# A graph network on one core: edge places computed in two pieces, and another division of labour for the masks of the second attention

## The chip, the cores and the metric

The kernel runs on one core of one Trainium2 chip. A core has a matrix engine (TensorE, PE in the profile; its weight loads are PEld), a vector engine (VectorE, DVE), a scalar engine (ScalarE, ACT), a general engine (GpSimd, POOL), a queue processor for transfers (SyncE, SP) and 16 DMA engines. The metric is the time of one execution on the device in microseconds.

## The reference, cut to what matters

There are 3125 nodes with 128 features, and 100,000 edges (`src`, `dst`, a weight, a type), sorted by `dst`. Four graph layers follow one another, each with a norm before it and a residual. The change touches what prepares the edges for all of them, and layer 0, two graph attentions:

```python
def gat_layer(x, W, a_s, a_d, b, src, dst):          # H = 4 heads of C = 32
    h = (x @ W).reshape(-1, H, C)
    al_src = jnp.einsum('nhc,hc->nh', h, a_s)
    al_dst = jnp.einsum('nhc,hc->nh', h, a_d)
    e = jax.nn.leaky_relu(al_src[src] + al_dst[dst], 0.2)
    m = jax.ops.segment_max(e, dst, num_segments=N)
    ...
    w = jnp.exp(e - m[dst])
    denom = jax.ops.segment_sum(w, dst, num_segments=N)
    alpha = w / jnp.maximum(denom[dst], 1e-16)
    out = jax.ops.segment_sum(h[src] * alpha[:, :, None], dst, num_segments=N)
    return out.reshape(-1, H * C) + b
x = jax.nn.relu(gat_layer(x, W1, a_src1, a_dst1, b1, src, dst))
x = jax.nn.relu(gat_layer(x, W2, a_src2, a_dst2, b2, src, dst))
```

## The kernel before, in words

**Blocks.** Nodes are cut into 25 blocks of 128 (`NB`). The edges become a dense matrix of edge counts, `counts` (source in the partition, target in the column, fp8), which stays in SBUF, and one of weights in DRAM. Gathers and segment sums are then matrix products.

**Placing the edges** (`place_edges`, L924 on). The edges are laid out as 112 partitions of 896 edges (`EC`; seven pieces of 128, `EK`). VectorE works out for each edge a row of a table in DRAM, so that the edges between one source block and one target block stand together: it compares the edge's block numbers, and a loop over 13 pairs of source blocks (L1019 to L1025: make a mask, scan along the row with a carry from the partition above, copy where the mask is set) gives the edge's rank among its like. Integer steps (L1027 to L1041) make the place `lane` out of it, with `cap` and `base`, two functions of the target block (L998 to L1011). L1043 to L1048 replace the places by plain numbers if the input is not as assumed; the test is a matrix product with ones into `ps_small`. Transposes (L1050 to L1056) make `idx` of it, the edge records are transposed into `rec` (L1058 to L1075), and GpSimd then issues 782 indirect transfers (L1081; the page's `table<-rec,idx`) of 128 edges each, one for each chunk `c` in the order `ORDER`, which begins with the chunks of target block 5. VectorE goes on with sums per target block (L1091), and `src` and `dst` are written out in another layout (L1113 to L1115).

**Building the graph and the first attention.** `graph_and_layer0` (L1376) interleaves, for the groups of blocks in `GROUPS` (blocks 5 to 24 in fours, then 0 to 2, then 3 and 4), `build_block` for each block with `attend(1, ...)` for the group. `build_block` loads the block's part of the table as soon as the scatters that can hold its edges are done, makes one-hot matrices on VectorE (L1174, L1176) and multiplies them (L1188, L1191).

**Attention on a group** (`attend`, L1318). The softmax's exponentials are products of a factor of the source and one of the target, with one pair of factors where the sum of the two scores is above zero and another where it is below. So for each head, source block `sb` and group, a mask `over` is made, the counts where `row > minus[sb]` and zero elsewhere: `row` is the targets' score, laid along the free axis in PSUM by TensorE transposes (`row_of`, tile `ps_row`), and `minus` holds the source's negated score, one per partition. TensorE multiplies each mask with the source's `parts` (L1349) into `ps_acc` over all 25 source blocks. Afterwards VectorE sums the three bf16 parts (L1354: the head's final sums), and a chain of VectorE operations (L1360 to L1373) at the end of the group makes the output. The same sum without a mask, `u`, comes from L1331 and L1333.

The second attention runs `attend(2, ...)` over five groups of five blocks (masks of 128x640), the first over the seven groups of `GROUPS` (128x512 at most). In the second, 6 of the 25 masks (`sb % 4 == 2`) are made by GpSimd in two operations, compare (L1341, `above`) and multiply (L1343); since GpSimd does not read PSUM here, `row_of` has ScalarE copy the row into SBUF (L1449). All other masks are one VectorE operation (L1346), which reads `ps_row` itself.

Each engine works in the order in which the kernel was written down, by the tile framework's semaphores: instructions on different engines that touch the same tile wait for one another, two readers of one PSUM tile included.

Of the kernel before, what the change touches and what calls it, by code (L numbers as in the profile page):

```python
# [7 lines left out]
F32 = mybir.dt.float32  # L8
# [51 lines left out]
FIRST = 5  # L60
ORDER = list(range(LOW[FIRST], ROWS)) + list(range(LOW[FIRST]))
GROUPS = [(q, q + 4) for q in range(FIRST, NB, 4)] + [(0, 3), (3, 5)]
# [836 lines left out]
class FastGnn(Gnn):  # L899
# [24 lines left out]
    def place_edges(self, placed):  # L924
# [9 lines left out]
        with ExitStack() as s:  # L934
# [63 lines left out]
            nc.scalar.copy(sb, sb_i)  # L998
            cap, base, step = tile("cap"), tile("base"), tile("step")
            V.tensor_scalar(cap, db, 24.0, 8.0, op0=OP.is_gt, op1=OP.mult)  # L1000
            V.tensor_scalar(cap, cap, 1.0, None, op0=OP.add)
            V.tensor_scalar(base, db, float(N_SLOTS[-1]), None, op0=OP.mult)
            for d in range(NB - 1):
                for _ in range(CAP[d] - CAP[d + 1]):
                    V.scalar_tensor_tensor(cap, db, d + 0.5, cap, op0=OP.is_lt, op1=OP.add)
                more = N_SLOTS[d] - N_SLOTS[d + 1]
                if more:
                    V.tensor_scalar(step, db, d + 1.0, float(more), op0=OP.min, op1=OP.mult)
                    V.tensor_add(base, base, step)
            V.tensor_tensor(step, sb, cap, op=OP.mult)  # L1010
            V.tensor_add(base, base, step)  # L1011

            left, wrong = tile("left"), work.tile([A, 2], F32, name="wrong")
            d0, d1 = tile("d0"), tile("d1")
            nc.scalar.copy(d0, raw["dst"])
            nc.scalar.copy(d1, raw["dst_next"])
            V.scalar_tensor_tensor(left, d0, 0.0, d1, op0=OP.add, op1=OP.is_gt, accum_out=wrong[:, :1])
            rank = tile("rank")
            V.memset(rank, 1.0)  # L1019
            for b in range(n_pair):  # L1020
                mask = hot.tile([A, EC], F32, name="mask")
                V.scalar_tensor_tensor(mask, pair, float(b), unit, op0=OP.is_equal, op1=OP.mult)
                run = hot.tile([A, EC], F32, name="run")
                V.tensor_tensor_scan(run, same, mask, carry[:, b : b + 1], op0=OP.mult, op1=OP.add)
                V.copy_predicated(rank, mask.bitcast(I32), run)  # L1025
            r_i, hi_i = tile("r_i", I32), tile("hi_i", I32)
            V.tensor_copy(r_i, rank)  # L1027
            whole_of(hi_i, r_i, OP.arith_shift_right, 12)
            whole_of(r_i, r_i, OP.bitwise_and, 4095)
            V.copy_predicated(r_i, odd_i, hi_i)  # L1030
            V.tensor_scalar(r_i, r_i, 1, None, op0=OP.subtract)
            r = rank
            V.tensor_copy(r, r_i)
            whole_of(hi_i, r_i, OP.arith_shift_right, 7)
            whole_of(r_i, r_i, OP.bitwise_and, 127)
            lane, level = tile("lane_f"), tile("level_f")
            V.tensor_copy(lane, r_i)
            V.tensor_copy(level, hi_i)
            V.tensor_add(level, level, base)
            V.scalar_tensor_tensor(lane, level, float(P), lane, op0=OP.mult, op1=OP.add)  # L1040
            V.tensor_scalar(lane, lane, float(TABLE - 1), 0.0, op0=OP.min, op1=OP.max)  # L1041

            V.scalar_tensor_tensor(left, cap, -float(P), r, op0=OP.mult, op1=OP.add)  # L1043
            V.tensor_scalar(left, left, 0.0, None, op0=OP.is_ge, op1=OP.add, accum_out=wrong[:, 1:])
            ps = psum.tile([P, P], F32, name="ps_small")
            nc.tensor.matmul(ps[:, :2], lhsT=self.ones[:A], rhs=wrong, start=True, stop=True)
            V.tensor_reduce(self.bad[:, 2:3], ps[:, :2], axis=AX.X, op=OP.add)
            V.copy_predicated(lane, bc(self.bad[:A, 2:3].bitcast(I32), [A, EC]), number)  # L1048


            idx = placed.tile([P, EK, A], I32, name="idx")
            for q, n in ((0, 4), (4, EK - 4)):
                ps = psum2.tile([P, 4, A], F32, name="ps_idx")
                for j in range(n):
                    nc.tensor.transpose(ps[:, j, :], lane[:, (q + j) * P : (q + j + 1) * P], self.ident[:A, :A])
                V.tensor_copy(idx[:, q : q + n], ps[:, :n])  # L1056

# [13 lines left out]
            for f, t in fields:  # L1071
                ps = psum2.tile([P, EK, A], BF16, name="ps_rec")
                for j in range(EK):
                    nc.tensor.transpose(ps[:, j, :], t[:, j * P : (j + 1) * P], self.ident16[:A, :A])
                nc.scalar.copy(rec_of[:, :, :, f], ps)  # L1075
# [3 lines left out]
            for c in ORDER:  # L1079
                p, k = divmod(c, EK)  # L1080
                st = nc.gpsimd.indirect_dma_start(  # L1081
                    out=self.table, out_offset=bass.IndirectOffsetOnAxis(ap=idx[:, k, p : p + 1], axis=0),
                    in_=rec[:, (k * A + p) * FIELDS :][:, :ROOM], in_offset=None)
                tc.declare_no_dep(st.ins, group=key, reason="each row has a place of its own")
                tc.add_to_no_dep_group(key, st.ins)
                self.placed[c] = st.ins


            sums = work.tile([A, NB], F32, name="sums")
# [228 lines left out]
    def attend(self, suffix, a, b, pools):  # L1318
# [9 lines left out]
        for q in range(n):  # L1328
            wide = u_tile()
            for sb in range(NB):  # L1330
                nc.tensor.matmul(wide[:, : HEADS * 3 * F1], lhsT=self.counts[:, sb, (a + q) * P : (a + q + 1) * P],  # L1331
                                 rhs=parts[:, sb, :, :, F1:], start=(sb == 0), stop=(sb == NB - 1))
            V.tensor_reduce(u[:, q], wide[:, : HEADS * 3 * F1].rearrange("p (h s f) -> p h f s", h=HEADS, s=3),  # L1333
                            axis=AX.X, op=OP.add)
        for i in range(HEADS):
            row, row_beside = row_of(lambda j: bc(self.sd[:, a + j, 1, i : i + 1], [P, P]), n)
            banks = [acc_tile() for _ in range(0, n, 2)]
            for sb in range(NB):
                if beside and sb % 4 == 2:
                    above = beside[0].tile([P, most * P], BF16, name="above0")  # L1340
                    nc.gpsimd.tensor_scalar(above[:, : n * P], row_beside, minus[:, sb, i : i + 1], None, op0=OP.is_gt)  # L1341
                    over = beside[1].tile([P, most * P], BF16, name="over")
                    nc.gpsimd.tensor_tensor(over[:, : n * P], above[:, : n * P], self.counts[:, sb, cols], op=OP.mult)  # L1343
                else:
                    over = stream.tile([P, most * P], BF16, name="over")
                    V.scalar_tensor_tensor(over[:, : n * P], row, minus[:, sb, i : i + 1], self.counts[:, sb, cols],  # L1346
                                           op0=OP.is_gt, op1=OP.mult)
                for j in range(n):
                    nc.tensor.matmul(banks[j // 2][:, j % 2, : 3 * F2], lhsT=over[:, j * P : (j + 1) * P],  # L1349
                                     rhs=parts[:, sb, i].rearrange("p s f -> p (s f)"),  # L1350
                                     start=(sb == 0 and j % 2 == 0), stop=(sb == NB - 1), skip_group_check=True)
            for q, ps in enumerate(banks):
                m = min(2, n - 2 * q)
                V.tensor_reduce(acc[:, 2 * q : 2 * q + m, i], ps[:, :m, : 3 * F2].rearrange("p d (s f) -> p d f s", s=3),  # L1354
                                axis=AX.X, op=OP.add)
# [19 lines left out]
    def graph_and_layer0(self, counts):  # L1375
# [3 lines left out]
        with ExitStack() as s:  # L1379
# [17 lines left out]
            with ExitStack() as s2:  # L1397
# [6 lines left out]
                def row_of(term, n):  # L1404
# [3 lines left out]
                    return ps[:, :n].rearrange("p a b -> p (a b)"), None  # L1408
# [19 lines left out]
            with ExitStack() as s2:  # L1428
                before = s2.enter_context(tc.tile_pool(name="l0_x", bufs=1))
                stream = s2.enter_context(tc.tile_pool(name="gat_c", bufs=8))  # L1430
                rows = s2.enter_context(tc.tile_pool(name="gat_d", bufs=2))
                done = s2.enter_context(tc.tile_pool(name="gat_o", bufs=2))
                beside = [s2.enter_context(tc.tile_pool(name=f"gat_b{n}", bufs=n)) for n in (1, 4)]
# [8 lines left out]
                def row_of(term, n):  # L1442

                    row = rows.tile([P, GW], F32, name="row")
                    ps = ps_row.tile([P, 8, P], F32, name="ps_row")
                    for j in range(n):
                        nc.tensor.transpose(ps[:, j, :], term(j), self.ident)
                    whole = ps[:, :n].rearrange("p a b -> p (a b)")
                    nc.scalar.copy(row[:, : n * P], whole)  # L1449
                    return whole, row[:, : n * P]  # L1450

                acc_tile = lambda: ps_acc.tile([P, 2, 256], F32, name="ps_acc")
                pools = (stream, done, lambda: acc_tile().rearrange("p a b -> p (a b)"), acc_tile, row_of, GB,
                         (beside[0], beside[1]))
# [467 lines left out]
```

## Time and profile before

| | us |
|---|---|
| median of three runs | 4500.81 (4499.46 to 4509.33) |
| profiled execution, its own time | 4494.62 |
| its span | 4492.8 |
| mean granted TensorE clock | 0.864 |

| stage | from | to |
|---|---|---|
| places of the edges | 0 | 140 |
| scatters, GpSimd | 140 | 1206 |
| graph and first attention | 1209 | 2305 |
| second attention | 2305 | 2746 |
| the other three layers | 2746 | 4493 |

Busy over the whole span: PE 60%, DVE 52%, PEld 43%, POOL 37%, ACT 15%. The largest shares belong to different stages, so each part of the change is to be read within its own stage. A time in a row of a timeline is from the span's start; the bracket at its end is the idle time before it on its engine and what ended it. A row with "x2" or more has several instructions of one kind together.

### The profile page before, as it was taken

What the parts mean: (1) busy time and instruction counts of PE and PEld (TensorE: products, weight loads), DVE (VectorE), ACT (ScalarE), POOL (GpSimd) and SP (SyncE); (2) the same over time, 40 slices, a digit from 0 to 9 for tenths busy, and PEclk for the clock granted to TensorE, in tenths of its full rate; (3) what the DMA queues carried; (4) which work ended last, traced back from release to release, by engine and by line L of the source; (5) the groups of instructions that cost most, each with busy time, mean ns of one, the idle gap of its engine ahead of it and who ended that gap; (6) DMA issues with size and microseconds to landing.
All of it is one profiled execution on the core that took longest, in us unless ns stands there. A gap on an engine that the chain in (4) does not pass through costs nothing.

```text
span 4492.8 us, 51542 instructions
## 1 busy us (share of the span) xinstructions
PE 2678.0 (60%) x20811; PEld 1911.4 (43%) x20811; DVE 2315.3 (52%) x3886; ACT 672.9 (15%) x1417; POOL 1670.6 (37%) x1474
## 2 busy tenths in 40 slices
PE   0110000000088878778878885988879994777777
PEld 0100000000056555556546663444455553677676
DVE  8602000000099999899988895011145563454545
ACT  0201000000024213402220001000021111222222
POOL 0577777777500000000049893000012104555552
PEclk9999655555599999999989998999989996889888
DMA  4000000000012111201000002776600003233332
GB/s 133 17 7 14 9 8 11 9 9 12 7 51 74 40 35 67 87 13 49 30 15 1 1 1 90 278 269 233 229 18 1 1 12 95 87 100 110 89 94 56
DMA packets 116938, 276.50 MB, mean 62 GB/s; under 512 B 27445, under 2 KB 67268, under 8 KB 105732
## 3 DMA queue, kind: packets, MB, share of 16 engines
q1 hardware_dynamic: 52182, 198.30, 13.1%
q0 software_dynamic: 37856, 32.76, 3.3%
q10 hardware_dynamic: 26652, 42.05, 2.6%
q8 instruction: 165, 2.70, 0.3%
q14 instruction: 83, 0.68, 0.0%
HBM read 210.00 MB, written 63.02 MB: 61 GB/s over the span
## 4 chain that ended last, share of the span: by engine, by line
PE 29%; DVE 26%; another core or an unknown queue 21%; issue 11%; POOL 7%; ACT 4%; DMA 2%; ACTq 0%; SPq 0%; DVEq 0%; POOLq 0%
PE ps_sum L531 9%; DVE over L1346 6%; DVE oh_w L1176 5%; POOL above L1341 4%; PE agg_wide L1782 3%; PE agg_far L1821 3%; PE ps_agg L1612 3%; PE ps_acc L1349 3%; POOL over L1343 2%; DVE oh_s L1174 2%; DVE oh_d L1174 2%; PE ps_m L1775 2%; PE ps_cw L1191 1%; ACT m_wide L1779 1%
## 5 line engine op out<-in xcount | busy, mean ns | idle before, releaser
L1081 POOL DMA_INDIRECT table<-rec,idx x782 | 818.0, 1046 | 378.6 <-issue 248.0
L1346 DVE SCALAR_TENSOR_TENSOR over<-ps_row,minus,counts 128x512 bf16<-128x512 f32 (+3 forms) x1080 | 729.5, 751 | 3.7 <-PE ps_acc L1349 1.9
L1349 PE MATMUL ps_acc<-parts,over 128*128 128x198 bf16 x5000 | 586.1, 250 | 172.3 <-POOL over L1343 67.5
L1341 POOL TENSOR_SCALAR above<-row,minus 128x640 bf16<-128x640 f32 x120 | 236.1, 1968 | 1112.6 <-ACT row L1449 1100.9
L1188 PE MATMUL ps_cw<-oh_d,oh_s 128*128 128x128 bf16 x1350 | 305.8, 229 | 518.9 <-remote 390.2
L1800 POOL DMA_INDIRECT m_far<-pre,src x401 | 395.8, 987 | 459.5 <-issue 262.7
L1349 PEld LDWEIGHTS <-over 128*128 128x128 bf16 x5000 | 385.3, 97 | 368.5 <-DVE over L1346 261.9
L1174 DVE TENSOR_TENSOR oh_s<-lane,keys 128x1024 bf16<-128x1024 bf16 (+2 forms) x187 | 118.3, 633 | 791.1 <-remote 747.9
L1191 PE MATMUL ps_cw<-oh_w,oh_d 128*128 128x128 bf16 x4050 | 403.8, 230 | 93.3 <-DVE oh_w L1176 47.5
L531 PE MATMUL ps_sum<-g,v_node 128*128 128x512 f32 (+1 forms) x1050 | 403.7, 547 | 1.9 <-ACT v_node L482 1.9
L1191 PEld LDWEIGHTS <-oh_d 128*128 128x128 bf16 x4050 | 315.6, 103 | 134.1 <-issue 113.4
L1188 PEld LDWEIGHTS <-oh_s 128*128 128x128 bf16 x1350 | 137.0, 102 | 548.7 <-issue 450.2
L1176 DVE TENSOR_TENSOR oh_w<-oh_s,keys 128x1024 bf16<-128x1024 bf16 (+2 forms) x561 | 325.0, 631 | 0.0
L1612 PE MATMUL ps_agg<-l_parts,counts 128*128 128x384 bf16 (+1 forms) x1875 | 315.8, 327 | 8.8 <-POOL l_parts L921 8.8
L1331 PE MATMUL ps_u<-parts,counts 128*128 128x396 bf16 x625 | 152.7, 356 | 281.7 <-issue 272.7
L1195 ACT ACTIVATE counts<-ps_cw 128x256 fp8e4<-128x256 f32 (+1 forms) x325 | 122.7, 378 | 1108.8 <-remote 781.3
L1782 PE MATMUL agg_wide<-m_wide,oh_wide 128*128 128x128 f32 x1100 | 187.9, 322 | 160.1 <-ACT m_wide L1779 107.3
L531 PEld LDWEIGHTS ps_sum<-g,v_node 128*128 128x128 f32 x1050 | 188.0, 190 | 218.2 <-issue 215.2
L1331 PEld LDWEIGHTS <-counts 128*128 128x128 fp8e4 x1250 | 112.7, 98 | 376.7 <-issue 292.7
L1612 PEld LDWEIGHTS <-counts 128*128 128x128 fp8e4 x1875 | 183.4, 98 | 133.5 <-issue 9.8
L1782 PEld LDWEIGHTS agg_wide<-m_wide,oh_wide 128*128 128x128 f32 x1100 | 160.6, 224 | 179.0 <-ACT m_wide L1779 125.3
L1494 DVE COPY v<-ps_sum 128x3200 f32<-128x3200 f32 x3 | 10.5, 3492 | 404.3 <-PE ps_sum L531 404.3
(349 smaller groups left out, 3597.4 us busy)
## 6 DMA issues: line engine op xcount, KB each, us to landing
g<-weights SPq DMA_DIRECT2D x75, 1600.0 KB
weights<-w_out ACTq DMA_DIRECT2D x150, 256.0 KB
src_row<-wide SPq DMA_DIRECT2D x32, 512.0 KB
table<-rec,idx POOLq DMA_INDIRECT x782
type_row<-wide SPq DMA_DIRECT2D x32, 384.0 KB
table<-none SPq DMA_DIRECT2D x1, 10864.0 KB
type_row<-types SPq DMA_DIRECT2D x25, 384.0 KB
m_far<-pre,src POOLq DMA_INDIRECT x401
```

Of the source, the lines that this page charges most:

```text
L531: nc.tensor.matmul(ps[:, c, :w], lhsT=y[:, b, :], rhs=flat[:, c0 : c0 + w], start=(b == 0), stop=(b == NB - 1))
L1081: st = nc.gpsimd.indirect_dma_start(out=self.table, out_offset=bass.IndirectOffsetOnAxis(ap=idx[:, k, p : p + 1], axis=0), in_=rec[:, (k * ...
L1174: nc.vector.tensor_tensor(oh[:, :h], bc(lane[:, None], wide), key(f), op=OP.is_equal)
L1176: nc.vector.tensor_tensor(oh_w[:, t, :h], oh_s[:, :h], key(WT + t), op=OP.mult)
L1188: nc.tensor.matmul(ps[:, 0, j, :], lhsT=oh_s[of], rhs=oh_d[of], start=(j == c == 0), stop=last, skip_group_check=True)
L1191: nc.tensor.matmul(ps[:, 1, j, :], lhsT=oh_d[of], rhs=oh_w[:, t][of], start=False, stop=(last and t == 2), skip_group_check=True)
L1341: nc.gpsimd.tensor_scalar(above[:, : n * P], row_beside, minus[:, sb, i : i + 1], None, op0=OP.is_gt)
L1346: V.scalar_tensor_tensor(over[:, : n * P], row, minus[:, sb, i : i + 1], self.counts[:, sb, cols], op0=OP.is_gt, op1=OP.mult)
L1349: nc.tensor.matmul(banks[j // 2][:, j % 2, : 3 * F2], lhsT=over[:, j * P : (j + 1) * P], rhs=parts[:, sb, i].rearrange("p s f -> p (s f)") ...
L1612: nc.tensor.matmul(ps[:, :n], lhsT=self.counts[:, sb, db * P : (db + 1) * P], rhs=parts[:, sb, :n], start=(sb == 0), stop=(sb == NB - 1))
L1782: nc.tensor.matmul(agg, lhsT=oh[:, j, :], rhs=m[:, j, :], start=(x == 0), stop=(x == n_slots - 1))
L1800: nc.gpsimd.indirect_dma_start(out=m[:, j, :], out_offset=None, in_=pre, in_offset=bass.IndirectOffsetOnAxis(ap=src_of[:, a + j : a + j + ...
```

## The change

Three things.

- **Places in two pieces.** Everything from `cap` to `idx` is done for the first four of the seven columns of 128 edges in each partition (512 wide), and then for the other three (384 wide); the scan of the second piece takes over the last column of the first by 13 small ScalarE copies into `carry`. `idx` becomes two tiles. The first 63 chunks of `ORDER` are sorted so that the 36 that lie in the first piece come first. The making of `rec` (splitting of the weights, casts, transposes, copies) is put ahead of the loop, its transposes and copies also in two pieces. The test with `ps_small` is made twice.
- **Two masks ahead.** In `attend`, in both attentions, the masks are made two source blocks ahead of the products that use them, and the final sums of a head (`sums`) come after the first two masks of the next head.
- **Other engines for the masks of the second attention.** For `sb % 3 == 2`, 8 of 25 masks, ScalarE compares, Sign of row plus the source's score, then Relu in place, and GpSimd multiplies by the counts. GpSimd's compare and the copy of the row are gone; the pools `gat_b1` and `gat_b4` become one with four buffers per tile, and `gat_d` goes.

```diff
+HALVES = ((0, 4), (4, EK - 4))
 ORDER = list(range(LOW[FIRST], ROWS)) + list(range(LOW[FIRST]))
+ORDER = [c for c in ORDER[: 9 * EK] if c % EK < 4] + [c for c in ORDER[: 9 * EK] if c % EK >= 4] + ORDER[9 * EK :]
...
+            nc.scalar.copy(sb, sb_i)
+            d0, d1 = tile("d0"), tile("d1")
+            nc.scalar.copy(d0, raw["dst"])
+            nc.scalar.copy(d1, raw["dst_next"])
+            for q, n in HALVES:
+                for f, t in fields:
+                    ps = psum2.tile([P, 4, A], BF16, name="ps_rec")
+                    for j in range(n):
+                        nc.tensor.transpose(ps[:, j, :], t[:, (q + j) * P : (q + j + 1) * P], self.ident16[:A, :A])
+                    nc.scalar.copy(rec_of[:, q : q + n, :, f], ps[:, :n])
...
+            for i, (q0, n0) in enumerate(HALVES):
+                lo, hi = q0 * P, (q0 + n0) * P
+                cut = lambda t: t[:, lo:hi]
+
+                cap, base, step, of_db = cut(t_cap), cut(t_base), cut(t_step), cut(db)
...
+                for b in range(n_pair):
+                    mask = hot.tile([A, 4 * P], F32, name="mask4")[:, : hi - lo]
+                    V.scalar_tensor_tensor(mask, cut(pair), float(b), cut(unit), op0=OP.is_equal, op1=OP.mult)
+                    run = hot.tile([A, 4 * P], F32, name="run4")[:, : hi - lo]
+                    V.tensor_tensor_scan(run, cut(same), mask, carry[:, b : b + 1], op0=OP.mult, op1=OP.add)
+                    V.copy_predicated(rank, mask.bitcast(I32), run)
+                    if hi < EC:
+                        nc.scalar.copy(carry[:, b : b + 1], run[:, hi - lo - 1 :])
...
+                of = placed.tile([P, n0, A], I32, name=f"idx{i}")
...
+                V.tensor_copy(of, ps[:, :n0])
+                for j in range(n0):
+                    idx[q0 + j] = of[:, j]
...
-                    out=self.table, out_offset=bass.IndirectOffsetOnAxis(ap=idx[:, k, p : p + 1], axis=0),
+                    out=self.table, out_offset=bass.IndirectOffsetOnAxis(ap=idx[k][:, p : p + 1], axis=0),
...
-            row, row_beside = row_of(lambda j: bc(self.sd[:, a + j, 1, i : i + 1], [P, P]), n)
-            banks = [acc_tile() for _ in range(0, n, 2)]
-            for sb in range(NB):
-                if beside and sb % 4 == 2:
-                    above = beside[0].tile([P, most * P], BF16, name="above0")
-                    nc.gpsimd.tensor_scalar(above[:, : n * P], row_beside, minus[:, sb, i : i + 1], None, op0=OP.is_gt)
-                    over = beside[1].tile([P, most * P], BF16, name="over")
-                    nc.gpsimd.tensor_tensor(over[:, : n * P], above[:, : n * P], self.counts[:, sb, cols], op=OP.mult)
+            row = row_of(lambda j: bc(self.sd[:, a + j, 1, i : i + 1], [P, P]), n)
+
+            def mask(sb):
+
+                if beside and sb % 3 == 2:
+                    above = beside.tile([P, most * P], BF16, name="above0")[:, : n * P]
+                    nc.scalar.activation(above, row, AF.Sign, bias=self.sd[:, sb, 0, i : i + 1])
+                    nc.scalar.activation(above, above, AF.Relu)
+                    over = beside.tile([P, most * P], BF16, name="over")
+                    nc.gpsimd.tensor_tensor(over[:, : n * P], above, self.counts[:, sb, cols], op=OP.mult)
                 else:
                     over = stream.tile([P, most * P], BF16, name="over")
                     V.scalar_tensor_tensor(over[:, : n * P], row, minus[:, sb, i : i + 1], self.counts[:, sb, cols],
                                            op0=OP.is_gt, op1=OP.mult)
+                return over
+
+
+            ready = [mask(0), mask(1)]
+            if sums:
+                sums()
+            banks = [acc_tile() for _ in range(0, n, 2)]
+            for sb in range(NB):
+                if sb + 2 < NB:
+                    ready.append(mask(sb + 2))
+                over = ready.pop(0)
                 for j in range(n):
                     nc.tensor.matmul(banks[j // 2][:, j % 2, : 3 * F2], lhsT=over[:, j * P : (j + 1) * P],
...
-            for q, ps in enumerate(banks):
-                m = min(2, n - 2 * q)
-                V.tensor_reduce(acc[:, 2 * q : 2 * q + m, i], ps[:, :m, : 3 * F2].rearrange("p d (s f) -> p d f s", s=3),
-                                axis=AX.X, op=OP.add)
+
+            def sums(i=i, banks=banks):
+                for q, ps in enumerate(banks):
+                    m = min(2, n - 2 * q)
+                    V.tensor_reduce(acc[:, 2 * q : 2 * q + m, i],
+                                    ps[:, :m, : 3 * F2].rearrange("p d (s f) -> p d f s", s=3), axis=AX.X, op=OP.add)
+        sums()
...
-                    whole = ps[:, :n].rearrange("p a b -> p (a b)")
-                    nc.scalar.copy(row[:, : n * P], whole)
-                    return whole, row[:, : n * P]
+                    return ps[:, :n].rearrange("p a b -> p (a b)")
```

## The prediction
> **What bounds the kernel now.** I read the table by stages first, then the chain of waits, then groups and timelines of the stages that the diff touches. Stage rows (us, then busy time of PE, PEld, DVE, ACT, POOL):
> ```profile
> 400.00:1209.00 809.00, 44.34 (x296) 30.74 (x296) 29.58 (x52) 14.20 (x37) 618.31 (x585) 0.56 0.05 9
> ...
> 2305.00:2746.00 441.00, 346.70 (x3139) 266.13 (x3136) 388.72 (x521) 17.83 (x29) 395.11 (x240) 0.99 0.02 5
> ```
> Until 1209 only GpSimd's 782 scatters make progress (DVE is busy 30 of 809 us); from 2305 to 2746, the second attention, GpSimd is the busiest engine. So the first scatter's time shifts all that follows, one to one. Timeline, DVE's rank loop and the first scatters:
> ```profile
> 85.19 1.07 DVE L1022 SCALAR_TENSOR_TENSOR mask<-pair,unit 112x896 f32<-112x896 f32 x1
> 86.17 1.16 DVE L1025 COPY_PREDICATED rank<-mask,run 112x896 f32<-112x896 int32 x1
> 87.22 2.08 DVE L1024 TENSOR_TENSOR_SCAN run<-same,carry,mask 112x896 f32<-112x896 f32 x1
> ...
> 140.16 1.14 POOL L1081 DMA_INDIRECT table<-rec,idx  x1 [130.53 <-ACT in_order L1114]
> 141.60 0.98 POOL L1081 DMA_INDIRECT table<-rec,idx  x1 [0.30 <-issue]
> ```
> DVE is gapless up to the indices; scatters then follow every 1.28 us (0.98 and 0.30 of issue).
>
> The chain within 2250 to 2760, then groups of 2416 to 2677, three inner groups of blocks (busy, mean ns, idle before):
> ```profile
> by line: POOL above L1341 31.2%; POOL over L1343 21.8%; DVE over L1346 12.5%; issue 7.3%; DVE acc L1354 2.4%; PE ps_acc L1349 2.1%; DVE u L1333 1.8%; DVE u L1367 1.7%; DVE u L1364 1.6%; DVE x L1371 1.5%; DVE r L1312 1.5%; DVE rest L919 1.5%
> ```
> ```profile
> L1346 DVE SCALAR_TENSOR_TENSOR over<-ps_row,minus,counts 128x640 bf16<-128x640 f32 x229 | 184.1, 874 | 0.0
> ...
> L1341 POOL TENSOR_SCALAR above<-row,minus 128x640 bf16<-128x640 f32 x73 | 145.1, 1987 | 7.2
> ...
> L1343 POOL TENSOR_TENSOR over<-above,counts 128x640 bf16<-128x640 bf16 x72 | 95.4, 1325 | 15.5 <-PE ps_acc L1349 9.7
> ...
> L1449 ACT COPY row<-ps_row 128x640 f32<-128x640 f32 x12 | 8.3, 692 | 206.1 <-PE ps_row L1447 206.1
> ```
> One inner group's window:
> ```profile
> 2502.88:2589.94 87.06, 72.21 (x648) 54.97 (x646) 78.25 (x105) 3.74 (x6) 79.55 (x49) 1.00 0.00 1
> ```
> GpSimd is busy 79.6 of 87.1, PE 72.2, DVE 78.3: a GpSimd mask comes every 3.39 us (starts 2414.48 and 2417.87), and 24 of them are 81.4 us. ScalarE is all but free.
>
> **Placement in two pieces.** The first indices now need 4 of 7 columns. Loop: starts in the rows are 0.98, 1.05 and 1.99 apart, 4.02 per bucket; less a fixed 0.08 each (what a 112x1 accumulator row costs), 3.78 x 384/896 = 1.62 leaves, x 13 buckets = 21. The other full-width steps ahead of the indices: seven STT, six TT and nine more at 0.98 to 1.05 shrink by about 0.4, some seventeen in the 0.62 us class by 0.2, 11 in all. The rec transposes, copies and casts move ahead of the loop, onto PE and ACT: six rec copies of 3.6 (one row has two in 7.14), now cut in twelve, and the casts are some 27 us of ACT beside a DVE that is busy to 109, so free; uncovered they would be those 27. Left at 128.65 to 139.3 now, they no longer end 0.8 after the indices; a second cast, three transposes and an L1091 row that got between save 2. Added ahead: about 3 us of moved splits and piece-2 steps that DVE takes in between. First scatter: 140.2 - 21 - 11 - 2 + 3 = **109**, so -31 (-28 to -32; -28 if the three splitting steps that now run inside the loop wait for edge_weight, SP's second load).
>
> Piece 2: 13 buckets at 384 wide (1.91 by the same rule) are 24.8, its other steps 14: 39 us. Cover: 36 scatters in piece 1, 46 us at 1.28. GpSimd should not wait; slack 7. The 13 carry copies on ACT lie between a scan and the *next* piece: not in the loop's way. But piece 2 now lies beside scatters, and the profile has a price for DVE beside scatters:
> ```profile
> 369.63 3.00 DVE L919 TENSOR_TENSOR rest<-r,parts 128x1320 f32<-128x1320 f32 x2
> ...
> 370.11 1.91 POOL L1081 DMA_INDIRECT table<-rec,idx  x1 [0.30 <-issue]
> ...
> 373.79 1.14 POOL L1081 DMA_INDIRECT table<-rec,idx  x1 [0.30 <-issue]
> ```
> From 367.2 to 391.3, beside DVE operations on two f32 tiles, 15 scatters take 1.6 us each, not 1.28; beside one-tile L1091 steps they keep 1.28. Piece 2 has both kinds: 24 scatters x 0.32 = 7.7 lost (0 to 15). The slowest of these rows is 2.2.
>
> The Trainium skill, "SBUF — State Buffer", section "SBUF: two separate sides", is harsher: a GpSimd-issued DMA of 620 ns took 3100 ns beside a 2-port VectorE copy, waiting for VectorE to end. By it 39 us would hold some 12 scatters, and the loss would be about 23, an estimate; the 1.6 us above speaks for less.
>
> The new order moves only the first 63 scatters among themselves. Block 5's table load on SP waits for all rows that block may have, the last of which now comes some 13 scatters (17 us) later; what is queued behind it is preparation that crawls anyway until 1209, so I price it with the next item. That preparation (the first blocks, with DVE busy 29.6 us in 809) has some 30 us less to crawl in and loses 2: the share 31/809 of its 44 us of PE, beside which DVE's 30 lie. Net: -31 + 7.7 + 2 = **-21.5** (-31.5 to -14).
>
> **Two masks ahead, first attention.**
> ```profile
> 1322.78 1.03 DVE L1354 TENSOR_REDUCE acc<-ps_acc 128x132 f32<-128x396 f32 x2
> 1323.73 16.54 DVE L1346 SCALAR_TENSOR_TENSOR over<-ps_row,minus,counts 128x512 bf16<-128x512 f32 x25
> ```
> DVE goes from sums to masks without a gap, 17.4 us a head, bound by its own 25 masks and two sums; an order with more masks ahead leaves that sum as it is: 0 (±2, if PE's end of a head shows).
>
> **Second attention.** Removed: GpSimd's compare (1.88) from 6 of 25 masks, and ACT's row copy (0.69, hidden). Added: per head 8 Signs from PSUM and 8 Relus on ACT, 8 multiplies of 1.33 on GpSimd (8 x 1.42 = 11.3 a head: no bound any more); DVE makes 17 masks, not 19. ACT has 8 x 1.5 = 12 a head: no bound by itself. But Sign reads the PSUM row that DVE's masks read, and in the instruction order the two take turns: Sign(sb) waits for DVE's mask sb-1, mask sb+1 for Sign(sb). Behind the waiting mask stand all of DVE's later masks, and PE behind these. One such turn is in the profile already:
> ```profile
> 2306.24 1.29 ACT L1449 COPY row<-ps_row 128x640 f32<-128x640 f32 x2 [1.66 <-DVE parts L921]
> ...
> 2306.96 0.89 DVE L1346 SCALAR_TENSOR_TENSOR over<-ps_row,minus,counts 128x640 bf16<-128x640 f32 x1 [0.56 <-ACT row L1449]
> ```
> DVE waits 0.56 for a 0.69 copy of the same row that began while it did a memset. A turn costs: mask latency 0.08 (alone 0.875, in a run 0.795: L1346's 14.33 us for 18), hand-over 0.10, Sign 0.70 (as the copy, same shape), back 0.03: 0.91.
>
> The Trainium skill's "PSUM — Partial Sum Buffer", section "PSUM bank collisions raise a hardware error", says that two engines may not be in one bank and quadrant at once, two readers included, and that dependencies keep them apart. It speaks against this change; the 0.56 us agrees. Without it, the sum would be the faster rival below.
>
> A head: 17 x 0.795 = 13.5; 7 turns x 0.91 = 6.4 (the eighth lies beside the three sums); the sums 1.2 (a row of three has 1.31); a wait of about 1.0 for PE at the end (Sign, Relu 0.74, multiply 1.33, ten matmuls for mask 23, against two masks of cover): 22.1, against 6 x 3.39 = 20.35. Four heads: 88.4 against 81.4, +7. A change of group: u's five sums, 0.48 apart, 2.4; ten chain operations, rows of 0.16 to 1.80, together 10.9, or 8.5 if those that are long beside GpSimd (L1364 1.78 for 660 columns, L1365 0.94 for 640) come half-way down; less five turns that run beside them 4.6: about 7.6 against 87.0 - 81.4 = 5.6, +2. So a period of **96**, and 5 x 7 + 4 x 2 = **+43** (+26 if Sign takes 0.58, the turn then 0.79; +53 if PE's wait is 1.5 a head).
>
> **Sum.** -21.5 + 0 + 43 = +21.5. The profiled execution (4494.62, span 4492.8) becomes 4516; it lies 6.2 below the median of the runs, so the forecast on the median's scale is 4500.8 + 21.5 = **4522**.
>
> **Rivals.**
> *A, faster: turns cost little.* If Sign and DVE's masks overlap or Sign is short, a group is bound by PE (72.2 and some 6 of waits, 78; DVE only 54.1 + 4.9 + 2.4 + 10.9 = 72.3). Then -9 x 5 = -45, with -21.5: -66, **4435**. It decides from the turn: 28 a group, so a group stays 87 at 0.91 - 9/28 = 0.59, and the whole breaks even at 0.91 - 4.7/28 = 0.74. For it: GpSimd is the bound and is relieved. Against: 2306.96.
> *B, no change:* both sizes at favourable ends: -31.5 + 26 = -5 to +9 (4496 to 4510).
> *C, slower yet: piece 2 misses its cover.* TensorE hand-overs during scatters show
> ```profile
> 474.76 0.38 ACT L1195 ACTIVATE counts<-ps_cw 128x256 fp8e4<-128x256 f32 x1 [35.75 <-remote]
> ```
> 36 us of waiting. Piece 2 has two TensorE steps (sum of wrong, index transposes); at 36 each its indices come after 39 + 72 = 111, against 36 x 1.6 = 57 of cover: GpSimd idles 53, in all **4575**. It decides once the two waits together exceed 18. Against: at 133 to 138, before the scatters, such a hand-over takes 1 to 2.
>
> **Numbers.** Forecast 0.62, A 0.10, B 0.20, C 0.08. Bounds: -31.5 + 26 = -5.5 and -14 + 53 = +39, with ±2 of the first attention and the runs' spread (-1.3, +8.5) about 4492 to 4545; A and C outside. 0.2% of this kernel, 9 us, is about what a measurement can tell. Faster by more: A and a sliver of B, 0.12; within: 0.18; slower: 0.70.
>
> **What would show it.** Right: first scatter near 109; the 37th without a long wait; last issue near 1181; in second attention, rows of DVE masks idle behind ACT's above0 by 0.7 to 0.8, Sign near 0.70, a group every 96, GpSimd busy about half; first-attention heads still 17.4. Wrong: scatter 37 late by tens of us (C); groups near 78 with PE gapless (A); Sign well below 0.6; heads of the first attention other than 17.4.

## The result and the profile after

The change makes the kernel slower: 4541.09 us median (4519.29 to 4556.34, 12 runs) against 4506.76 (4499.46 to 4518.63, 12 runs), ratio 1.0065, 95% interval 1.0053 to 1.0078. That is 34 us, or 0.65%; 21.5 us were forecast, and the time lies within the stated range of 4492 to 4545, near its upper end. The span of the profiled execution (4530.0) is 37.2 longer than that of before. The two profiles are taken apart in what follows.

Placement first. Timeline of the kernel after: a stretch of VectorE's loop over the second piece and of the scatters beside it, and the last scatter (start, duration, engine, line, in brackets the idle time before):
```profile
108.15 1.26 POOL L1096 DMA_INDIRECT table<-rec,idx  x1 [98.50 <-DVE cap L1042]
...
118.83 1.00 DVE L1055 TENSOR_TENSOR_SCAN run<-same,carry,mask 112x384 f32<-112x384 f32 x1
119.06 1.55 POOL L1096 DMA_INDIRECT table<-rec,idx  x1 [0.30 <-issue]
119.75 0.53 DVE L1053 SCALAR_TENSOR_TENSOR mask<-pair,unit 112x384 f32<-112x384 f32 x1
120.20 0.58 DVE L1056 COPY_PREDICATED rank<-mask,run 112x384 f32<-112x384 int32 x1
120.67 1.00 DVE L1055 TENSOR_TENSOR_SCAN run<-same,carry,mask 112x384 f32<-112x384 f32 x1
120.91 1.54 POOL L1096 DMA_INDIRECT table<-rec,idx  x1 [0.30 <-issue]
...
135.68 0.97 POOL L1096 DMA_INDIRECT table<-rec,idx  x1 [0.30 <-issue]
...
1180.11 1.09 POOL L1096 DMA_INDIRECT table<-rec,idx  x1 [0.30 <-issue]
```
The first scatter comes at 108.15 (140.16 before). From 115.37 to 135.68 scatters go at VectorE's pace: scan to scan 1.84, scatter to scatter 1.85, one scatter for each turn of the loop, eleven in all. With the five ahead of them, sixteen take 27.5 us, where 1.28 each would make 20.5. Scatter 37 waits for nothing but the usual 0.30 of issue. The last one, at 1205.13 before, comes 25.0 earlier.

Second attention: an inner group's window, three groups' rows and their waits (line waited for: total us, times, longest):
```profile
2392.58:2491.76 99.18, 79.53 (x648) 60.45 (x646) 72.25 (x96) 49.71 (x68) 42.80 (x32) 0.91 0.00 1
```
```profile
L1365 DVE SCALAR_TENSOR_TENSOR over<-ps_row,minus,counts 128x640 bf16<-128x640 f32 x204 | 171.0, 877 | 70.3 <-ACT above L1359 70.3
...
L1362 POOL TENSOR_TENSOR over<-above,counts 128x640 bf16<-128x640 bf16 x96 | 128.4, 1338 | 168.9 <-ACT above L1360 152.6 <-PE ps_acc L1379 15.0 <-issue 1.3
L1359 ACT ACTIVATE above<-ps_row,sd 128x640 bf16<-128x640 f32 x97 | 77.0, 793 | 140.6 <-DVE over L1365 140.6
```
```profile
ACT above L1359 <- DVE over L1365: 140.6, 97, 4.5
PEld L1379 <- POOL over L1362: 82.6, 84, 2.7
DVE over L1365 <- ACT above L1359: 70.3, 81, 0.9
```
VectorE's masks, which had no idle time in front of them before, now wait 81 times for Sign, 0.87 each, and Sign waits for them. PE's weight loads wait 82.6 us for the masks that GpSimd finishes, so late masks could be the cause as well; e4 below decides. The period from group to group is 99.1 instead of 87.0, while GpSimd is busy for 43 and not 80. The timeline shows the turns:
```profile
2410.71 1.32 DVE L1386 TENSOR_REDUCE acc<-ps_acc 128x132 f32<-128x396 f32 x3 [1.33 <-PE ps_acc L1379]
...
2421.51 0.79 ACT L1359 ACTIVATE above<-ps_row,sd 128x640 bf16<-128x640 f32 x1 [1.04 <-DVE over L1365]
...
2422.34 0.74 ACT L1360 ACTIVATE above<-above 128x640 bf16<-128x640 bf16 x1
2422.34 1.68 DVE L1365 SCALAR_TENSOR_TENSOR over<-ps_row,minus,counts 128x640 bf16<-128x640 f32 x2 [0.92 <-ACT above L1359]
...
2424.11 0.79 ACT L1359 ACTIVATE above<-ps_row,sd 128x640 bf16<-128x640 f32 x1 [1.04 <-DVE over L1365]
```
Two masks, Sign, two masks: 2.60 us for three source blocks. Two masks in a run are 1.59, so a turn costs 1.01. From sums to sums (2410.71, then 2433.19, 2455.66, 2478.12, 2509.80) a head takes 22.47, and 31.7 where the group changes.

The books, between ends of stages: VectorE's last `x` of the first attention comes at 2247.5 instead of 2268.0, 20.5 gained. From there to the last `x` of the second attention it takes 536.7 instead of 478.5, 58.2 lost. The rest of the kernel is equal within 0.7.

### The profile page after: what moved, and what is told of

The parts are those of the page before. It is cut to its first block, busy times and chain, and to the rows that moved or that the text cites. A ratio compares the mean times of both kernels' runs of the same rounds, so it can differ in the third digit from the quotient of the medians.

```text
span 4530.0 us, 51988 instructions
## 1 busy us (share of the span) xinstructions
PE 2707.2 (60%) x20813; PEld 1933.7 (43%) x20813; DVE 2299.5 (51%) x3925; ACT 905.0 (20%) x1736; POOL 1499.1 (33%) x1394
## 5 line engine op out<-in xcount | busy, mean ns | idle before, releaser
L1096 POOL DMA_INDIRECT table<-rec,idx x782 | 830.1, 1062 | 341.4 <-issue 242.9
L1365 DVE SCALAR_TENSOR_TENSOR over<-ps_row,minus,counts 128x512 bf16<-128x512 f32 (+3 forms) x1040 | 709.4, 747 | 122.7 <-ACT above L1359 119.0
L1379 PE MATMUL ps_acc<-parts,over 128*128 128x198 bf16 x5000 | 613.8, 262 | 193.8 <-POOL over L1362 102.9
L1362 POOL TENSOR_TENSOR over<-above,counts 128x640 bf16<-128x640 bf16 x160 | 213.5, 1335 | 1379.6 <-ACT above L1360 1350.0
L1379 PEld LDWEIGHTS <-over 128*128 128x128 bf16 x5000 | 414.7, 102 | 393.1 <-DVE over L1365 216.5
```

What stands on the lines that cost most here:

```text
L1096: st = nc.gpsimd.indirect_dma_start(out=self.table, out_offset=bass.IndirectOffsetOnAxis(ap=idx[k][:, p : p + 1], axis=0), in_=rec[:, (k * ...
L1362: nc.gpsimd.tensor_tensor(over[:, : n * P], above, self.counts[:, sb, cols], op=OP.mult)
```

## The experiments

The experiments ran after the first pair, on three chips (numbered 14, 12 and 11; for the first pair no number is known). There the kernel before takes 3344 to 3346 us instead of 4507, and all ratios below are against it on the same chip. Of the difference, 938 us lie ahead of the end of the first group of the first attention, beside GpSimd's indirect transfers, and about 213 in the last three layers. PE's one-hot products on the page of before, and on the page of the changed kernel in e5:
```profile
L1188 PE MATMUL ps_cw<-oh_d,oh_s 128*128 128x128 bf16 x1350 | 305.8, 229 | 518.9 <-remote 390.2
```
```profile
L1204 PE MATMUL ps_cw<-oh_d,oh_s 128*128 128x128 bf16 x1350 | 299.0, 224 | 48.4 <-ACT w_out L1212 24.9
```
390 us of waiting that the profile calls "remote" are gone. Blocks are built while scatters run, and the first group of the first attention ends near 430 instead of 1368. The second attention's period is the same on both sides, 87.0 before and 99.0 after, so its verdicts carry over. Those on the places have to be read for each side.

**The parts alone.** e1 is the kernel before with the diff's places, e2 with its attention, e5 the change itself.

```diff
e1: hunks of HALVES, ORDER and place_edges only
e2: hunks of attend, row_of and the pools only
e5: all
```


> The kernel before with the places in two pieces alone; attention as before. Theory (the parts add up, and each is what its stage shows): first scatter near 108, last near 1180, dense work 25 us earlier, second attention with its period of 87.0 us, total 20 to 25 us below the kernel before, ratio 0.9945 to 0.9956. Rival (the 4.6 us by which the first attention's stage grew come from two masks ahead, not from less preparation between scatters): the stage from the first dense row to the last x of the first attention is 1034 us as before, and all 25 us arrive; by the theory it is 1039 and 20.5 arrive. Rival (placement beside scatters costs more than it saves): 0 or slower.

> The kernel before with the changed attention (two masks ahead, Sign and Relu on ScalarE, multiply on GpSimd) and the places as before. Theory: second attention's period 99 us, that stage 58 us longer than before, total +58 to +63, ratio 1.013 to 1.014; together with the places alone it gives the changed kernel. Rival (the later start of ScalarE's and GpSimd's work matters, parts interact): the two do not add up to within 8 us.

> The changed kernel itself, beside the kernel before on the chip of these experiments, where everything from the scatters to the last layer runs quicker. Theory (the change is the sum of its parts: places -26.6, masks +57.6): +31 us, ratio 1.008 to 1.011; second attention's period 99.1 as in the first profile; the first group of the first attention ends 24 to 25 us earlier than with the places in one piece (430.5), where the first profile of the change had lost 5 of its 25 us by that point. Rival (the parts interact beside scatters): the sum misses by over 8 us.

Measured: e1 3319.41 against 3346.01, ratio 0.9924 (0.9910 to 0.9938), -26.6; e2 3403.64, 1.0173 (1.0159 to 1.0187), +57.6; together +31.0. e5 3377.51 against 3344.33, 1.0101 (1.0086 to 1.0117), +33.2. The parts add up to within 2.2. The last scatters of e1 and of e2, which has the places of before, each with the end of the first group of the first attention (ScalarE's last step on `x`):
```profile
1120.42 0.96 POOL L1096 DMA_INDIRECT table<-rec,idx  x1 [0.30 <-issue]
405.56 0.63 ACT L1389 ACTIVATE x<-x 128x512 f32<-128x512 f32 x1 [0.77 <-DVE x L1388]
```
```profile
1145.04 0.97 POOL L1081 DMA_INDIRECT table<-rec,idx  x1 [0.31 <-issue]
430.45 0.63 ACT L1390 ACTIVATE x<-x 128x512 f32<-128x512 f32 x1 [0.81 <-DVE x L1389]
```
The last scatter is 24.6 earlier, as in the first pair, and the first group 24.9, so here all of it arrives, with two masks ahead (e5: 405.0) or without (e1). The first pair lost 5 of its 25 us in the first group: from the first one-hot row of the gapless stretch (1233.72 before, 1208.61 after) to the group's `x` it takes 134.8 and 140.2. Its traces show where. From that row to the first block's sum `u` are 8.3 us before and 14.4 after, two sets of one-hot rows more, because less of the block was done between the scatters. Block 5's table load there waits for VectorE's `parts` and comes at 514.98 instead of 393.13. Why so much later stays open, since no experiment repeated the conditions of the first pair.

**The turns, or late masks.** e4 is the change with Sign reading an SBUF copy of the row.

```diff
+                row = rows.tile([P, GW], F32, name="row")        # rows: bufs=1; stream: bufs=7
...
+                    nc.scalar.copy(row[:, : n * P], whole)
+                    return whole, row[:, : n * P]
...
-                    nc.scalar.activation(above, row, AF.Sign, bias=self.sd[:, sb, 0, i : i + 1])
+                    nc.scalar.activation(above, row_beside, AF.Sign, bias=self.sd[:, sb, 0, i : i + 1])
```


> The changed kernel, but ScalarE first copies the row to SBUF once a head and its Signs read the copy (one buffer; VectorE's masks have 7 buffers instead of 8 to make room), so that Sign and VectorE's masks no longer share a PSUM tile. Theory (the loss is the turn-taking on the row: 28 turns of about 1.0 us a group): VectorE's masks run back to back, the rows 'idle <- ACT above' are gone, the period falls from 99 to 75 to 82 us, total 85 to 120 us below the changed kernel, 4420 to 4455. Rival (the masks of ScalarE and GpSimd are late, Sign, Relu and multiply of 2.9 us against two masks of cover, and TensorE waits for them whatever VectorE does): period 92 or more, total within 35 us of the changed kernel.

Measured: 3248.48, ratio 0.9710 (0.9697 to 0.9723): 97.5 us below before and 129 below the change, more than the 85 to 120 of the theory. (The total of 4420 to 4455 had been written for the speed of the first pair; the difference is what counts.) Window of an inner group, and rows of three:
```profile
1422.40:1497.00 74.60, 69.82 (x647) 55.34 (x646) 68.60 (x97) 47.75 (x70) 41.88 (x32) 1.00 0.01 1
```
```profile
L1365 DVE SCALAR_TENSOR_TENSOR over<-ps_row,minus,counts 128x640 bf16<-128x640 f32 x204 | 164.1, 876 | 0.6 <-ACT row L1481 0.6
L1379 PE MATMUL ps_acc<-parts,over 128*128 128x198 bf16 x1500 | 142.1, 248 | 14.3 <-DVE over L1365 7.7 <-POOL over L1362 4.2
...
L1359 ACT ACTIVATE above<-row,sd 128x640 bf16<-128x640 f32 x96 | 74.9, 815 | 1.1
```
The same engines do the same eight compares, relus and multiplies a head, and a copy more, and the period falls from 99.1 to 74.6, of which PE is busy 69.8 and VectorE 68.6. VectorE's 70.3 of idle time have become 0.6. The turns were the whole loss and more, and the late-mask theory falls: PE's products wait for GpSimd 4.2 us in three groups, its weight loads 6.6 instead of 82.6. GpSimd's masks had been late because Sign was. Sign takes 0.815 from SBUF, no less than from PSUM, so it was the sharing that cost, not its length.

**The order.** e3 has two masks ahead with GpSimd's masks of before; e6 is the change and e7 is e4, both without the masks ahead.

```diff
-            ready = [mask(0), mask(1)]        # e6, e7; sums directly after the head's last product
...
-                if sb + 2 < NB:
-                    ready.append(mask(sb + 2))
-                over = ready.pop(0)
+                over = mask(sb)
```


> The kernel before with two masks ahead and the final sums after them, nothing else: GpSimd compares and multiplies 6 of 25 masks as before, ScalarE copies the row. Theory: GpSimd bounds the second attention at 3.39 us a mask, which the order leaves; period 84 to 87 us, first attention's heads 17.4 us, total 0 to -15 against the kernel before. Rival (the order itself costs, since a head's sums and with them its PSUM banks come later): period above 90, total +15 or more, and the loss of the changed kernel is then partly the order's.

> The changed kernel without the two masks ahead: each mask is written down just before its products, and a head's sums after its last product. Sign, Relu and multiply for 8 of 25 masks, and the turns on the row, stay. Theory (the turns set the period, the order adds little once GpSimd is no bound): period 97 to 103, total within 20 us of the changed kernel. Rival (the order is what costs, as it cost 5.8 us a group with GpSimd's masks): period 92 to 94, total 25 us or more below the changed kernel.

> Sign from an SBUF copy of the row, without the two masks ahead. With the masks ahead the period was 74.6, of which PE was busy 69.8. Theory (PE is the bound, so that the order moves at most PE's 4.8 idle us): period 72 to 77, total within 15 us of the copy with masks ahead, 0.966 to 0.976 of the kernel before. Rival (two masks of cover are what let ScalarE's and GpSimd's masks come in time): period 82 or more.

Measured: e3 3366.04, ratio 1.0063 (1.0049 to 1.0077), period 92.8: its rival was right, the order by itself costs 5.8 a group. e6 has 3377.64, 1.0096 (1.0081 to 1.0112), period 99.1, and e7 3251.63, 0.9723 (0.9709 to 0.9736), 74.6: both as with masks ahead. Timelines of e3 at a change of group, PE's row transposes and GpSimd:
```profile
1452.97 0.27 PE L1463 MATMUL ps_row<-ident,sd 128*128 128x128 f32 x1
...
1482.01 1.15 PE L1463 MATMUL ps_row<-ident,sd 128*128 128x128 f32 x9
```
```profile
1475.69 1.32 POOL L1345 TENSOR_TENSOR over<-above,counts 128x640 bf16<-128x640 bf16 x1
1483.59 1.88 POOL L1343 TENSOR_SCALAR above<-row,minus 128x640 bf16<-128x640 f32 x1 [6.58 <-ACT row L1465]
```
Five transposes make a row. In before all five of the group's second row stand ahead of the products for `u` (at 2389.88). In e3 one does (1452.97), and the others come only with the third row's, after the first head's last product; GpSimd, the bound, waits 6.58 for it once a group, which is about the 5.8. Why the schedule splits that row was not followed further. Where GpSimd is no bound (e6, e7), the same order costs nothing.

**The places.** e9 is before with the records' making moved ahead alone; e8 and e10 are e4 with other pieces.

```diff
e9:  block from 'w = raw["edge_weight"]' to the rec copies moved ahead of 'cap', one piece
e8:  HALVES = ((0, 3), (3, 2), (5, 2))   # ORDER's first 63 sorted by piece
e10: HALVES = ((0, 3), (3, EK - 3))      # likewise
```


> The kernel before with the making of the records (weights split, casts, transposes, copies) written down ahead of the loop, and nothing else; places in one piece. Theory (the 32 us come from the two pieces; the records had already been hidden beside VectorE): first scatter 0 to 3 us earlier than 140.6, total within 4 us of the kernel before. Rival (the records' way ahead is what brought much of it): first scatter 10 us earlier or more, total 8 us or more below.

> Sign from an SBUF copy of the row, with the places in three pieces of 3, 2 and 2 columns and the first 63 chunks sorted accordingly. Theory (the first indices wait for their own columns alone): 13 buckets of 1.62 x 128/384 = 0.54 and other steps of about 3.5 less, so the first scatter 10 us earlier, near 98; the second piece, some 27 us, has 27 scatters of 1.7 to 1.85 us as cover, so GpSimd does not wait; total 4 to 10 us below the copy in two pieces, since scatters run at 1.85 us for longer. Rival (the steps that do not shrink with the width, and DVE shared with scatters, eat it): first scatter 104 or later, or a wait at scatter 28, total the same or longer.

> Sign from an SBUF copy, places in two pieces of 3 and 4 columns instead of 4 and 3. Theory (with 4 and 3, VectorE's own work up to the first one-hot row, 239 us, has become the bound on this chip, not the scatters): first scatter 6 to 8 us earlier, near 101; VectorE's total is the same, so the first group of the first attention ends at 403 to 407 as before and the total is within 4 us of the copy with 4 and 3. Rival (the scatters still set the start): the first group ends 6 us or more earlier and the total falls as much; or GpSimd waits at scatter 28, 27 scatters being too little cover for the larger second piece.

Measured: e9 3341.79 against 3343.95, ratio 0.9992 (0.9983 to 1.0001), first scatter 138.0, 2.6 earlier: the pieces bring the gain, not the move. e8 has 3264.22, 0.9762 (0.9749 to 0.9776), 16 slower than e4, though its first scatter, at 100.5, is 8 earlier and its last 12. e10 has 3280.80, 0.9805 (0.9791 to 0.9818), 32 slower than e4, first scatter 102.5. I had expected no loss from either, and both theories failed. e8's rival has the longer total, but neither the late first scatter nor the wait at scatter 28 that it put it down to; e10's rival, a group that ends earlier, failed too. e10's timeline, SyncE's wait, and block 5's table load in e10 and e4:
```profile
123.40 0.73 DVE L1056 COPY_PREDICATED rank<-mask,run 112x512 f32<-112x512 int32 x1
124.02 1.28 DVE L1055 TENSOR_TENSOR_SCAN run<-same,carry,mask 112x512 f32<-112x512 f32 x1
125.20 0.67 DVE L1053 SCALAR_TENSOR_TENSOR mask<-pair,unit 112x512 f32<-112x512 f32 x1
125.24 2.08 POOL L1096 DMA_INDIRECT table<-rec,idx  x1 [0.30 <-issue]
```
```profile
SPq L1167 <- DMA table<-rec,idx: 81.4, 4, 76.4
```
```profile
264.29 0.30 SPq L1167 DMA_DIRECT2D slots<-table  x1
```
```profile
233.15 0.30 SPq L1167 DMA_DIRECT2D slots<-table  x1
```
Again one scatter a turn, now every 2.39. But the larger loss is in the last rows: the load of block 5's table waits for scatters until 264.29 (e4: 233.15), when GpSimd has issued 106 (e4: 88), and the first group ends 32.4 later (438.3, e4: 405.9). In e8 the same load comes at 249.14, 16.0 later than in e4, and the group ends 15.0 later. A theory for this: the schedule as built does not keep the written order of the scatters, other than was said of the engines above. Chunks of the first piece past the first 63 slip in while the second piece is not ready, so that block 5's last chunk is no longer among the first 63. e11 and e12 hold them back:

```diff
+            zero = work.tile([P, 1], I32, name="zero")            # from the second piece's indices
+            V.tensor_scalar(zero, last[:, 0, :1], 0, None, op0=OP.mult)
+            every = placed.tile([P, HALVES[0][1], A], I32, name="every")
+            for k in range(HALVES[0][1]):
+                V.tensor_tensor(every[:, k], idx[k], bc(zero, [P, A]), op=OP.add)
...
+                of = idx[k] if c in ORDER[: 9 * EK] or k >= HALVES[0][1] else every[:, k]
```


> The copy with pieces of 3 and 4 columns, its scatters held to the written order: chunks past the first 63 take the first piece's places from a second tile, which VectorE writes only once the second piece's indices are there (a sum with zero of the second tile; seven small int32 operations; VectorE's masks of the second attention get 6 buffers instead of 7 to make room). Theory (3 and 4 lost 32 us because first-piece chunks past the first 63 slip ahead of the second piece, so that block 5's load waits for some 105 scatters instead of 54): block 5's table load near 235 instead of 264, first group of the first attention ends at 402 to 410 instead of 438, total 25 to 35 us below 3 and 4. Rival (what costs is scatters that run at one per bucket of VectorE's wider loop, 2.39 us): group ends at 425 or later, total within 10 us of 3 and 4.

> The same hold with the change's own pieces of 4 and 3 columns and Sign from the copy. Theory (block 5's load, at 233, waited 5 us for VectorE's parts and 49 for scatters, the last of them near the 83rd; held to the 57th, VectorE's parts alone release it, and block 8's 133rd scatter is as before): first group ends 0 to 5 us earlier than 405.9, total within 6 us of the copy without the hold, ratio 0.968 to 0.973. Rival (the hold makes GpSimd wait for the second piece, or adds to VectorE's path): 6 us or more longer.

Measured: e11 3252.58 against 3344.98, ratio 0.9725 (0.9711 to 0.9738), 28 below e10; the first group ends at 412.1 instead of 438.3, 2 later than the theory had it and far from its rival's 425. e12 has 3250.52, 0.9717 (0.9704 to 0.9731), group's end 405.8 as in e4. SyncE's waits in e11 up to 236:
```profile
SPq L1174 <- DVE parts L923: 45.9, 1, 45.9
...
SPq L1174 <- DMA table<-rec,idx: 8.6, 2, 7.3
```
Block 5's load (237.03) now waits for VectorE's own preparation. e11 has the slow scatters of e10 still, 2.39 apart, so these were not the loss: 28 of e10's 32 us were the slip. e8's loss looks the same by its load, but no run held its scatters back. In e12 the load comes at 234.23, after 44.8 us of waiting for VectorE, and e4's, which waits for scatters, comes no later. So with 4 and 3 columns the start of the dense work hangs on VectorE as much as on scatters here, and an earlier first scatter (e8, e10, e11) brought nothing.

## Why the prediction was right

| step | forecast | measured |
|---|---|---|
| first scatter | 109 | 108.15 |
| scatters slowed beside piece 2 | 7.7 | 7.1 |
| wait at scatter 37 | none | none |
| last scatter | near 1181 | 1180.11 |
| net of the places, at the first attention's end | -21.5 | -20.5 |
| first attention, between the first groups' ends | unchanged | 159.8, as before |
| Sign, turn | 0.70, 0.91 | 0.79, 1.01 |
| a head, period | 22.1, 96 | 22.47, 99.1 |
| second attention | +43 | +58.2 |

**Direction and mechanism** held: the turns on the PSUM row, read off one wait of 0.56 us, are the loss, and e4 shows that without them the kernel is faster than before. The point of decision held too: the turn, 1.01, is above 0.74. Rival A's mechanism came true in e4: with no turns a group takes 74.6 (forecast 78), 69.8 of it busy PE, with VectorE close behind.

The Trainium skill, "PSUM — Partial Sum Buffer", section "PSUM bank collisions raise a hardware error", has the reason for keeping two readers of a bank apart: reading it at once raises an error. The trace shows them kept apart, by 81 waits of 0.87.

**Term mis-sized: the second attention**, 43 for 58. Sign was priced like the row copy, 0.692; it takes 0.793, in all forms seen here longer than the copy. 28 turns of 0.10 more are 2.8 of the 3.1 by which the period was too short. Two other terms about cancel: PE's wait at the end of a head was 0.59 and not 1.0, and a change of group took 9.2 more than a head, not 7.6. Three such periods make 9 of the 15 us that are missing. The last group has 8 more: +15.3 (79.1 to 94.4), where I had +7. I took GpSimd's 24 masks as that group's time, 81.4, yet GpSimd makes the first of them ahead, beside the group before, as the heads of before show: 30.0 from sums to sums over a change, then 16.2, 20.3 and 20.5. The first group takes 2 back, +6.8 where the sum has +9.

**Steps that were wrong without showing in the time.** I wrote that the new order moves only the first 63 scatters among themselves, and that block 5's last chunk comes 13 scatters later. The schedule moves others past them, as e10 and e11 show. In the first pair it held nothing up: block 5's load there waits for VectorE's `parts` (255.1 us of waiting), not for scatters. The preparation that crawls between the scatters was charged 2 us and lost 4.5; the first scatter, a little earlier than forecast, made up part of it.

I also gave the masks ahead no price in the second attention, and no reason for that. With GpSimd as the bound they cost 5.8 a group (e3); in the change, where it is no bound, they cost nothing, with the turns (e6) or without (e7). So the zero was right, without a reason given, which is luck.

Three sums of the prediction do not come out, none of them by much. The upper bound, added as it stands, is 4550 and not 4545. A bucket of the second piece is 1.86 by the rule given, not 1.91 (1.84 were measured). The turn at which the whole breaks even, 21.5 us over five groups of 28 turns below 0.91, is 0.76, not 0.74.

**Slow scatters** were right in their total, 7.1 us against 7.7, but partly by luck: 24 scatters at 1.6 were taken, and sixteen at 1.72 on average were measured, after which the pace was 1.28 again. They were wrong in kind, for eleven of them keep step with VectorE's loop, at 1.85 for 384 columns (2.39 for 512, in e10). The Trainium skill, "SBUF — State Buffer", section "SBUF: two separate sides", describes a transfer blocked until VectorE ends rather than one that shares. The locked step fits that, while the price worked out from the page, an estimated 23 us, was three times the 7.1 measured. The page's numbers are for a VectorE copy; which of the loop's three operations blocks here was not separated.

**Not foreseen:** that until 1209 almost only scatters progress is a property of the first pair's executions, not of the kernel. What the "remote" waits are, and whether the chip makes the difference, stays open. The places brought the last scatter 25 us forward on either side, of which 20.5 arrived in the first pair and all in the experiments. There the dense work starts at the scatters' end, here a group's table loads wait for its own scatters or for VectorE.

## What to carry to other kernels

Before work is handed to an idle engine, look at which tile it reads. Here the engine that shared the work read the same PSUM tile, the two took turns, and a short wait in the old trace gave nearly the price of a turn (0.91 taken, 1.01 measured). One copy of the operand to SBUF per head turned a loss of 58 us into the best ratio of this study, 0.971. Where a scheduler picks what is ready, work split to start early can let later pieces slip ahead of what a consumer waits for; follow the consumer's load, not the first start.

## What the runs showed of the hardware that I had not expected

The same kernel took 4507 us in one series of executions and 3344 to 3346 in others, on three chips. In the first, hand-overs to and from TensorE beside GpSimd's indirect transfers show tens of us of "remote" waiting (390 us in front of the one-hot products alone); no page of the others has such a row. The reason was not found.

GpSimd's indirect transfers kept step with VectorE's loop of mask, scan and predicated copy: one for each turn, every 1.85 us at 384 columns and 2.39 at 512, against 1.28 alone.

ScalarE's Sign with a bias takes 0.79 us for 128x640 f32 from PSUM and 0.815 from SBUF, a plain copy of the same row from PSUM to SBUF 0.69.
